# Output projections in seven half-block products: an attention kernel on one TensorE

## The chip, the cores and the metric

The kernel runs on one core of a Trainium2 chip. A core has five engines, each with its own instruction stream: TensorE (PE in the profile) multiplies matrices and writes PSUM, VectorE (DVE) and ScalarE (ACT) work elementwise and may read PSUM, GpSimd (POOL) works elementwise on SBUF, and SyncE (SP) here issues nearly all DMA transfers. The engines wait for one another through semaphores. Each engine runs its own stream strictly in order, so an instruction that waits holds up everything behind it.

The metric is the time of one execution in microseconds on the device. All numbers are f32.

## The reference

One layer: layer norm, cross attention with 8 heads over a context of 3202 rows, a residual, a second layer norm, a small recurrence over time, and a second residual. Cut to what matters here:

```python
x = _layernorm(builder_state, g1, beta1)             # 4096 x 512
base_n = _layernorm(base_state, g1, beta1)           # 3202 x 512
x = residual + _mha(x, base_n, W_qkv, b_qkv, W_o, b_o)   # ends with out @ W_o.T + b_o
xn = _layernorm(x, g2, beta2)
U = (xn @ W_in.T + b_in) @ Bmat
def step(s, u_t):
    s = jax.nn.silu(s @ A.T) + u_t
    return (s, s)
# states over the 4096 rows, then x + states @ Cmat + a row that depends on ctxb
```

The change concerns `out @ W_o.T`: 4096 x 512 by 512 x 512.

## The kernel before

*Stages.* For the first 200 us the kernel normalizes the context and computes keys and values, which go to DRAM. Then comes the attention of 64 units: a unit is 256 queries (a half of a block of 512) by a pair of heads (`hp`, 0 to 3). There are 8 blocks `Q`, and in each but the last the units run pair by pair, both halves of a pair in turn. A unit goes through the context in 13 chunks of 256 keys (`NDC`). At the end, a recurrence over the rows and the last outputs remain.

*One chunk.* `scores` (L1095) is 16 matmul instructions on 64x64 tiles of the array, into one of two PSUM tiles `s`. ACT takes the exponential into a tile `p` of SBUF (`weights`, L1172, `NP` = 15 tiles in a ring). `product` (L1229) multiplies it by the values, 16 instructions, four steps later (`LAG`), and DVE adds `p` into a sum (`add`, L1180). After 13 chunks a unit's output is copied to a tile `o` (L1274), joined (L1278), and scaled by the inverse of the sum (reciprocal L1301, `scale` L1312).

*Projections of the queries.* For the next block these run in `by_sevenths`: the 512x512 product is split into four quarters, and seven products of half size replace eight (Strassen's scheme in Winograd's form). The differences of the weights (`query_weights`) are made once; three to four sums of the other side (`tq`, L1468) are made per block. `seventh` (L364) is one product: 4 matmuls of 128x128 by 128x256, which the profile lists as 8 instructions, because an f32 matmul is two. The seven go in the order `CHAIN` = 1 2 6 5 7 3 4 into two PSUM banks x and y. A bank holds running sums: after some products an engine reads it (`READS`: four by ACT at L1491, three by DVE at L1487) before the next product adds to it.

*Projections of the outputs.* `project` does a half of a block in one piece `outs` (L1561): for each of two tiles of 128 rows, 4 matmuls of 128x128 by 128x512, 16 instructions in all. Then per tile DVE adds the residual (`x1`, L1574), to which POOL has added the bias (`row`, L1555); the second layer norm follows, POOL adds a further row (`mod`, L1578), DVE turns it (`flip`, L441), DMAs move the parts into place (`move`), and PE makes 64 inputs of the recurrence (`inputs`, L1618; `kept`).

*What sets the order.* All work from the attention on is added to a `Plan` as pieces: engine, cost in ns, the pieces it comes after, a due time, and the ring buffers that it takes and gives (`p`, `m` for two PSUM tiles, `x`, `x1`, `o_` and so on). `Plan.order` simulates the engines with these costs and takes, whenever an engine is free, the ready piece that is due first. `SHIFT` moves the due times of a kind of piece by multiples of `STEP` = 2150 ns. For PE, pieces of kind "quarters" (64x64 tiles) and those on the full array are told apart: a change between them costs `ENTER` or `LEAVE`, full-array pieces are kept together (`KEEP`), and a lone one is put off (`ALONE`). The order that comes out is written as the program of each engine; at run time only semaphores decide. The chunks of K and V are loaded by SP 10 and 6 steps ahead.

*The end.* `drain` plans it: the last half's projection (L1881), its rows, a sweep "a" and a sweep "b" of the recurrence over most rows, a recurrence of 20 dependent steps for the last rows (L1966 on ACT, L1969 on DVE), and 16 row tiles that are fetched, added to and stored. Row tiles 0 to `NA` - 1 lie in `alt` tiles, the others in the ring `p`.

Of the kernel before, what the change touches and what calls it, by code (L numbers as in the profile page):

```python
# [20 lines left out]
P = 128  # L21
# [20 lines left out]
NP = 15  # L42
NA = 3
# [28 lines left out]
class Plan:  # L72
# [8 lines left out]
    ENTER, LEAVE = 110, 147  # L81
# [3 lines left out]
    PORT = ("add", "rest", "fold", "gather", "scale", "t", "tq", "tied", "wk", "wv", "wq", "rowv")  # L85

    SHIFT = {
        "row.store": 11.5, "fold": 2, "rows.outs": 0.75, "heads": -12, "sample": -3, "spread": 4.75,
        "query.flip": -11, "states": -5.5, "inverse": 4.75, "extra": 10, "scale": -57.75, "rest": -1,
        "row.mod": -17, "joined0": -14.25, "b": -15, "add.l": -23, "l.stats": -34.75, "last": -4.5,  # L90
        "base": -34.75, "inverse.l": -27, "rows.inputs": 3.5, "maximum": -13.5, "fall": -19, "query.stats": -8,
        "den": 4.5, "row.scaled": 12, "l.h": -7, "row.stats": -9.25,
    }

    def __init__(self, rings, held):
# [19 lines left out]
    def order(self):  # L115
# [26 lines left out]
        while len(out) < len(pieces):  # L142
            for e in self.LATE:
# [24 lines left out]
                free[e] = now + cost  # L168
                if shares(p):
                    port = free[e]  # L170
                heapq.heappush(events, (free[e], 0, p["at"], p))
                heapq.heappush(events, (free[e] + self.LATE[e], 1, p["at"], p))
# [5 lines left out]
            while events and events[0][0] <= now:  # L178
                _, late, _, p = heapq.heappop(events)
                if late:  # L180
                    for g in p["give"]:
                        givers[g] -= 1
# [10 lines left out]
def xattn_ssm_kernel(  # L193
# [886 lines left out]

    def parts_of(t):
# [3 lines left out]
    o_t = {}  # L1085
# [194 lines left out]
    def finish(w, i, d, plan):  # L1280
# [33 lines left out]
        plan.add(("output", i), "ACT", 360, partial(output, w), [("product", i, NDC - 1)], d, ["o_"])  # L1314
# [6 lines left out]
        else:  # L1321
            plan.add(("fold", i), "DVE", 680, partial(fold, w), [("add", i, NDC - 1)], d + 500)
            plan.add(("swap", i), "ACT", 760, partial(swap, w), [("fold", i)], d + 600, ["rd"])
            plan.add(("gather", i), "DVE", 860, partial(gather, w), [("swap", i)], d + 700, [],
                     [("rd", ("swap", i))])
            plan.add(("sums", i), "PE", 300, partial(sums, w), [("gather", i), from_(d + 8 * STEP)], d + 1000,
                     ["m", "m"], acc, "quarters")
            opened = ("den", i, 0)
            for k in range(2):
                plan.add(("den", i, k), "ACT", 450, partial(denominators, k),  # L1330
# [19 lines left out]
    def norm_pieces(plan, ks, gets, d, after, names, gives, wait):  # L1350
# [21 lines left out]
        for t, (k, v) in enumerate(zip(ks, vs)):  # L1372
            plan.add((*k, "stats"), "DVE", 870, partial(stats_, v, gets[t], names[t]),
                     [after[t]] + ([(*ks[0], "stats")] if t else []),
# [1080 lines left out]
```

## Time and profile before

| | |
|---|---|
| Median of 3 runs | 1912.18 us (1912.11 to 1913.63) |
| The profiled execution | 1913.58 us |
| its span, first to last instruction | 1911.7 us |
| granted TensorE clock, mean | 0.998 |
| PE / DVE / ACT / POOL busy | 1895.2 / 1535.3 / 1176.6 / 237.7 us |
| output projections (L1561) on PE | 107.0 us |

A row of the timeline gives start, length, engine, line, operation, the output and input tiles, the shape, and how many instructions were merged (x16); in brackets stands the idle time of the engine just before it and what ended it. A row of a group gives the count, the time that the group kept its engine busy, the mean length of one in ns, and the idle time before them with what ended it. In a window's row stand its length, then per engine the busy time and number of instructions (PE, PEld for weight loads, DVE, ACT, POOL), the granted clock, the share of DMA and GB/s. A row of the waits gives who waited for whom, the total, the number of times and the longest.

### The profile page before, as it was taken

Reading aid. Unit: us, or ns where it says so; the run is one execution under the profiler, and the core shown is the slowest. Engines: PE = TensorE matmul, PEld = TensorE weight load, DVE = VectorE, ACT = ScalarE, POOL = GpSimd, SP = SyncE. Lnnn points to the kernel's source line nnn. Section 1 sums busy time; section 2 is a strip of 40 time slices with the busy share of each in tenths; the row PEclk is TensorE's granted clock in tenths of the full one; section 3 lists DMA queues with packets and bytes.
Section 4 is the critical chain, followed back from the end, with each engine's and each line's share of the span. In section 5 each row is a group of like instructions: output and inputs, shape, how many; then the busy total and the mean of one; then the engine's idle time right before and its main releaser. Section 6 shows DMA issues by size and latency. Waiting matters only on the chain.

```text
span 1911.7 us, 68126 instructions
## 1 busy us (share of the span) xinstructions
PE 1895.2 (99%) x29464; PEld 1352.6 (71%) x29464; DVE 1535.3 (80%) x2084; ACT 1176.6 (62%) x1675; POOL 237.7 (12%) x382
## 2 busy tenths in 40 slices
PE   9999999999999999999999999999999999999997
PEld 5887679766677667766777667766776677766675
DVE  6642699788879889788878887888978887988876
ACT  3242677576666666656757665766756775756653
POOL 6120000001100120011000120012001110011105
PEclk9999999999999999999999999999999999999999
DMA  7554233132422343224413242234322341544577
GB/s 254 156 158 123 63 102 88 45 101 77 110 71 84 92 126 93 81 75 112 110 41 93 81 121 75 82 89 122 101 68 75 96 122 46 160 120 133 175 197 224
DMA packets 260764, 207.50 MB, mean 109 GB/s; under 512 B 94632, under 2 KB 233896, under 8 KB 260460
## 3 DMA queue, kind: packets, MB, share of 16 engines
q1 hardware_dynamic: 256440, 196.48, 36.6%
q10 hardware_dynamic: 4020, 6.62, 1.1%
q8 instruction: 233, 3.82, 0.9%
q14 instruction: 71, 0.58, 0.1%
HBM read 156.32 MB, written 29.88 MB: 97 GB/s over the span
## 4 chain that ended last, share of the span: by engine, by line


## 5 line engine op out<-in xcount | busy, mean ns | idle before, releaser
L1172 ACT ACTIVATE p<-s,shifts 128x1024 f32<-128x1024 f32 (+1 forms) x832 | 892.9, 1082 | 481.1 <-PE s L1095 464.0
L1180 DVE TENSOR_TENSOR acc<-p,acc 128x1024 f32<-128x1024 f32 (+1 forms) x704 | 829.1, 1178 | 119.8 <-ACT p L1172 85.9
L1095 PE MATMUL s<-q,k 64*64 64x256 f32 x12800 | 837.4, 377 | 0.2 <-ACT p L1172 0.2
L1229 PE MATMUL po<-p,v 64*64 64x256 f32 x12800 | 837.4, 377 | 0.0
L1095 PEld LDWEIGHTS s<-q,k 64*64 64x64 f32 x12800 | 499.9, 133 | 199.5 <-ACT p L1172 16.4
L1229 PEld LDWEIGHTS po<-p,v 64*64 64x64 f32 x12800 | 496.4, 133 | 177.1 <-issue 12.9
L1555 POOL TENSOR_TENSOR xr<-xr,rowb 128x512 f32<-128x512 f32 x30 | 41.3, 1390 | 994.3 <-DMA xr<-in_x_dram 467.4
L1301 DVE RECIPROCAL rd<-rd 128x256 f32<-128x256 f32 (+1 forms) x64 | 110.2, 1723 | 23.5 <-ACT rd L1296 23.5
L1561 PE MATMUL pa<-wo,o 128*128 128x512 f32 x240 | 107.0, 599 | 0.0
L1180 DVE TENSOR_TENSOR acc<-p,p 128x1024 f32<-128x1024 f32 x64 | 78.2, 1222 | 10.9 <-ACT p L1172 10.6
L1561 PEld LDWEIGHTS pa<-wo,o 128*128 128x128 f32 x240 | 44.4, 190 | 56.0 <-issue 56.0
L1204 DVE TENSOR_TENSOR acc<-swap,acc 64x256 f32<-64x256 f32 x126 | 56.7, 450 | 8.9 <-ACT swap L1199 7.0
L1166 DVE TENSOR_TENSOR acc<-x,acc 2x256 f32<-2x256 f32 x128 | 55.0, 430 | 2.5
L1199 ACT COPY swap<-acc 64x256 f32<-64x256 f32 x126 | 50.8, 403 | 6.5 <-DVE acc L1187 3.4
L1578 POOL TENSOR_TENSOR xr<-x,modb 128x512 f32<-128x512 f32 x30 | 38.2, 1273 | 116.9 <-DVE x L1574 116.9
L1491 ACT ACTIVATE q<-qx,bias 128x256 f32<-128x256 f32 x42 | 17.6, 471 | 45.8 <-PE qx L364 45.8
L542 DVE TENSOR_TENSOR ks<-pky,ks 128x512 f32<-128x512 f32 x15 | 10.4, 692 | 43.6 <-PE pky L364 28.7
L1362 POOL TENSOR_SCALAR rstd_x<-mv_x 128x1 f32<-128x1 f32 x28 | 6.2, 221 | 313.5 <-DVE mv_x L1359 311.8
L536 ACT ACTIVATE ks<-pkx,bias 128x256 f32<-128x256 f32 x40 | 16.8, 471 | 45.0 <-PE pkx L364 33.6
L1187 DVE TENSOR_TENSOR acc<-acc 128x512 f32<-128x512 f32 x63 | 43.2, 686 | 1.4
L1278 DVE TENSOR_TENSOR o<-po,o 128x256 f32<-128x256 f32 x64 | 27.0, 421 | 12.3 <-ACT o L1274 7.6
L1129 DVE TENSOR_REDUCE m<-sm 128x1 f32<-128x256 f32 x64 | 24.1, 419 | 15.7 <-PE sm L1115 15.2
(283 smaller groups left out, 1588.8 us busy)
## 6 DMA issues: line engine op xcount, KB each, us to landing
k<-kd SPq DMA_DIRECT2D x432, 128.0 KB, 2.4
v<-vd SPq DMA_DIRECT2D x432, 128.0 KB, 2.3
xn<-x SPq DMA_DIRECT2D x448, 32.0 KB, 1.9
xr<-in_x_dram SPq DMA_DIRECT2D x30, 256.0 KB, 3.4
x1d<-xr SPq DMA_DIRECT2D x30, 256.0 KB, 2.5
x<-in_x_dram SPq DMA_DIRECT2D x28, 256.0 KB, 4.0
cx<-in_ctx_dram SPq DMA_DIRECT2D x25, 256.0 KB, 4.3
kd<-ks SPq DMA_DIRECT2D x20, 256.0 KB, 2.3
```

The source lines that it names most:

```text
L1095: nc.tensor.matmul(s[k0 : k0 + HD, a, b, :], kts[(*w["at"][:2], c)][r, b * CK + k0 : b * CK + k0 + HD], q[r], start=True, stop=True, skip_ ...
L1166: nc.vector.tensor_tensor(to[r], t[r], to[r], ALU.add)
L1172: nc.scalar.activation(t[:, :, :nb, :], w["ps"][c][:, :, :nb, :], AF.Exp, bias=w["shift"])
L1180: nc.vector.tensor_tensor(w["acc"][:, :, :nb, :], t[:, :, :nb, :], before[:, :, :nb, :], ALU.add)
L1187: nc.vector.tensor_tensor(acc[:, :, 0, :], acc[:, :, 0, :], acc[:, :, 1, :], ALU.add)
L1199: nc.scalar.copy(w["swap"][r], of[(1 - k) * HD : (2 - k) * HD])
L1204: nc.vector.tensor_tensor(of[r], w["swap"][r], of[r], ALU.add)
L1229: nc.tensor.matmul(w["po"][k][a * HD : (a + 1) * HD, :QU], vts[Q, hp, c][r, b, a * HD : (a + 1) * HD], t[r, a, b, :], start=(c == 0 and b ...
L1301: nc.vector.reciprocal(w["rd"][:, part], (w["pd"] if last else w["rd"])[:, part])
L1555: nc.gpsimd.tensor_tensor(v["x"], v["x"], rowb, ALU.add)
L1561: nc.tensor.matmul(v["pa"], o_t[Q, c, half][:, t * P : (t + 1) * P], wo[:, c, :], start=(c == 0), stop=(c == NC - 1),)
L1578: nc.gpsimd.tensor_tensor(v["x"], v["x1"], modb, ALU.add)
```

## The change

Three things change.

The output projections of blocks 0 to 6 no longer go through `project`, half by half, but through `project_by_sevenths`, once per block of 512 rows, as seven products. The left side (the attention outputs, in quarters: two halves by two pairs of heads) needs four sums on DVE, two of them written over quarters that are not needed any more; the right side (`wo`) needs four differences, made once by POOL (`output_weights`). The seven products go into two PSUM banks, and DVE reads after each of the seven, adding into the residual rows (L1574's four additions per block go). The rows after it (norm, turn, moves, inputs) are in `rows_pieces`, the second half `HALF` = 18 steps behind the first. `project` keeps the first half of the last block; the last half of it is in `drain` as before.

The output tiles lie in pairs of heads, so that two neighbours form a quarter: 6 pairs in place of 12 halves. Five more `alt` tiles hold the differences of `wo`, one half's `x1` and every third `x` tile (the ring `x` grows from 2 to 3), and `p` falls from 15 to 11 tiles.

The planner's costs are set anew (a few in the diff below), `Plan` takes a time `OVER` by which an engine is free before an operation has ended, and `SHIFT` has 65 entries in place of 28. The first half of the next block's query rows is loaded and normalized `EARLY` = 13 steps sooner.

```diff
-NP = 15
-NA = 3
+NP = 11
+NA = 7
+HALF = 18
+EARLY = 13
+OUTS = 0
...
-    ENTER, LEAVE = 110, 147
+    OVER = {"DVE": 80, "ACT": 100}
+    ENTER, LEAVE = 200, 280
...
-        "row.store": 11.5, "fold": 2, "rows.outs": 0.75, "heads": -12, "sample": -3, "spread": 4.75,
...
+        "row.store": 11.5, "fold": 5, "rows.outs": 12.25, "heads": -12, "sample": 1, "spread": -6.25,
...
+        "row.move3": 1, "l.from": -5, "l.copy": -12, "l.states": -8, "l.turn": -4, "row.flip": 4.5,
+        "swap.l": -4, "l.near": 4, "differ": -0.5, "row.load": 12, "add": 16, "rest.l": -8, "den.l": 12,
...
-                free[e] = now + cost
+                free[e] = now + cost - (self.over.get(e, 0) if cost > 200 else 0)
...
+    def x_tile(name):
+
+        x_tiles.append(name)
+        if len(x_tiles) % 3 == 1:
+            return alt_tile(6, name)
+        return xp_.tile([P, 2, H], F32, tag="x", name=name)
...
-        o = o_t[Q, hp, half] = op.tile([P, QU], F32, tag="o", name=f"o_{w['name']}", bufs=12)
+        if hp % 2 == 0:
+            t = op.tile([P, 2, QU], F32, tag="o", name=f"o_{w['name']}", bufs=6)
+            for k in range(2):
+                o_t[Q, hp + k, half] = t[:, k]
+            o_pairs[Q, hp // 2, half] = t
+        o = o_t[Q, hp, half]
...
-            plan.add(("sums", i), "PE", 300, partial(sums, w), [("gather", i), from_(d + 8 * STEP)], d + 1000,
+            plan.add(("sums", i), "PE", 225, partial(sums, w), [("gather", i), from_(d + 8 * STEP)], d + 1000,
...
+        d -= EARLY * STEP
...
+    def output_weights(plan, after, d):
+
+        b11, b21, b12, b22 = quarters(wo)
+        right, tiles = rights, {}
+        right.update(zip("123", (b11, b21, b22)))
+
+        def sum_(k, x, y):
+            if k in "57":
+                tiles[k] = parts_of(alt_tile(3 + "57".index(k), f"to{k}"))
+            right[k] = tiles["57"[k in "74"]][k in "64"]
+            x, y = (right[z] if isinstance(z, str) else z for z in (x, y))
+            nc.gpsimd.tensor_tensor(right[k], x, y, ALU.subtract)
+
+        for i, (k, x, y) in enumerate((("5", b12, b11), ("6", b22, "5"), ("7", b22, b12), ("4", b21, "6"))):
+            plan.add(("to", k), "POOL", 1300, partial(sum_, k, x, y),
+                     [("to", "567"[i - 1])] if i else after, d + i * STEP)
...
+    def project_by_sevenths(plan, Q, d, index):
+
+        index = {(c, half): index[Q, c, half] for c in range(NC) for half in range(2)}
+        v, xs, x1s, left = {}, {}, {}, {}
+        key, k2s = ("outs", Q), [("rows", Q, half) for half in range(2)]
+        kss = [[("row", Q, half * 2 + t) for t in range(2)] for half in range(2)]
+        ats = [[Q * QB + half * QU + t * P for t in range(2)] for half in range(2)]
+
+        def load(half, t):
+            if t == 0:
+                xs[half] = x_tile(f"xr_{ats[half][0]}")
+            at = ats[half][t]
+            nc.sync.dma_start(xs[half][:, t], x[at : at + P, :])
+
+        def row(half, t):
+            nc.gpsimd.tensor_tensor(xs[half][:, t], xs[half][:, t], rowb, ALU.add)
+
+        for half in range(2):
+            for t in range(2):
+                k = kss[half][t]
+                first = (*kss[half][0], "load")
+                plan.add((*k, "load"), "SP", 800, partial(load, half, t),
+                         [first] if t else [from_(d - 6 * STEP)], d - 6 * STEP + 2 * half + t, [] if t else ["x"])
+                plan.add((*k, "row"), "POOL", 1270, partial(row, half, t),
+                         [(*k, "load"), from_(d - 2 * STEP)], d - STEP)
+
+        def parts():
+            return [o_pairs[Q, pair, half] for half in range(2) for pair in range(2)]
+
+        def open_left():
+            a11, a12, a21, a22 = v["a"] = parts()
+            left.update(zip("124", (a11, a12, a22)))
+            left["7"], left["3"] = a21, a12
+
+        def sum_(k):
+            if k == "5":
+                left["5"], left["6"] = parts_of(alt_tile(2, f"so_{Q}"))
+            a11, a12, a21, a22 = v["a"]
+            x, y, op = {
+                "5": (a21, a22, ALU.add), "6": (left["5"], a11, ALU.subtract),
+                "7": (a11, a21, ALU.subtract), "3": (a12, left["6"], ALU.subtract),
+            }[k]
+            nc.vector.tensor_tensor(left[k], x, y, op)
+
+        def product_(k):
+            if k == "1":
+                open_left()
+                v["x"], v["y"] = (
+                    m_tile([P, 512], f"pa{n}_{Q}").rearrange("p (b k) -> p b k", b=2) for n in "xy"
+                )
+            seventh(v["y" if k in "235" else "x"], left[k], rights[k], k in "125")
+
+        def read(k):
+            m, n = (int(z) - 1 for z in READS[k][0])
+            of, cs = v["y" if k in "235" else "x"], slice(n * QU, (n + 1) * QU)
+            if k == "1":
+                x1s[0] = xp_.tile([P, 2, H], F32, tag="x1", name=f"x1_{ats[0][0]}", bufs=1)
+            elif k == "5":
+                x1s[1] = alt_tile(5, f"x1_{ats[1][0]}")
+            t = x1s[m][:, :, cs]
+            nc.vector.tensor_tensor(t, of, xs[m][:, :, cs] if k in "1654" else t, ALU.add)
+
+        def o_of(pair, half):
+            return ("o_", ("output", index[2 * pair, half]))
+
+        def scales(pair, half):
+            return [("scale", index[2 * pair + k, half], 0) for k in range(2)]
+
+        a11, a12, a21, a22 = [(pair, half) for half in range(2) for pair in range(2)]
+        used = {"5": (a21, a22), "6": (a11,), "7": (a11, a21), "3": (a12,)}
+        for k in "5673":
+            after = {"5": scales(*a21) + scales(*a22) + [(*key, "1")], "6": [("so", Q, "5")],
+                     "7": [("so", Q, "5")], "3": [("so", Q, "6"), (*key, "2")]}[k]
+            plan.add(("so", Q, k), "DVE", 690, partial(sum_, k), after, d, ["tq"] if k == "5" else [],
+                     [o_of(*z) for z in used[k]] + ([("tq", ("so", Q, "5"))] if k in "63" else []))
+        before = {"6": "1", "5": "2", "7": "6", "3": "5", "4": "7"}
+        needs = {
+            "1": scales(*a11) + [("to", "4")] + [(*k, "row") for ks in kss for k in ks],
+            "2": scales(*a12) + [(*key, "1")], "4": scales(*a22),
+        }
+        gives = {
+            "1": [o_of(*a11)], "2": [o_of(*a12)], "3": [o_of(*a12)], "4": [o_of(*a22)], "7": [o_of(*a21)],
+            "5": [("tq", ("so", Q, "5"))], "6": [("tq", ("so", Q, "5"))],
+        }
+        last_scale = scales(*a22)
+        for at, k in enumerate(CHAIN):
+            after = needs.get(k, [("so", Q, k)]) + ([("outs.read", Q, before[k])] if k in before else [])
+            plan.add((*key, k), "PE", 1740, partial(product_, k), after + last_scale,
+                     d + STEP * 3 // 4 + at - (plan.ALONE if at > 1 else 0),
+                     ["m", "m"] if k == "1" else [], gives[k])
+            plan.add(("outs.read", Q, k), "DVE", 690, partial(read, k), [(*key, k)], d + at,
+                     {"1": ["x1"], "5": ["x1b"]}.get(k, []), [("m", (*key, "1"))] if k in "34" else [])
+        done = [("outs.read", Q, k) for k in "23"], [("outs.read", Q, k) for k in "74"]
+        for half in range(2):
+            vs = [dict(x=None) for _ in range(2)]
+            free = ("x1b", ("outs.read", Q, "5")) if half else ("x1", ("outs.read", Q, "1"))
+            rows_pieces(plan, Q, half, d + half * HALF * STEP, vs, lambda half=half: (xs[half], x1s[half]), done[half], free, 12)
...
+    def rows_pieces(plan, Q, half, d, vs, tiles, done, free, gate):
...
+        nv = norm_pieces(plan, ks, [lambda t=t: tiles()[1][:, t] for t in range(2)], d + STEP, [done] * 2,
+                         [f"y{r}" for r in at], [], [from_(d + gate * STEP)])
...
+        plan.add((*k2, "inputs"), "PE", 850, inputs, copied + [from_(d + (gate + 12) * STEP)],
+                 d + 16 * STEP, ["m"], [("xn2", xn2)])
...
-            plan.add(("weights", i, c), "ACT", 200 + 861 * part, partial(weights, w, c),
+            plan.add(("weights", i, c), "ACT", 286 + 828 * part, partial(weights, w, c),
...
-                plan.add(("add", i, c), "DVE", 120 + 1120 * part, partial(add, w, c),
+                plan.add(("add", i, c), "DVE", 135 + 1090 * part, partial(add, w, c),
...
-                s=2, m=2, mt=1, o=1, p=NP, acc=3, extra=4, q=3, tq=1, x=2, x1=1, xn2=1, fs=4,
-                xn=1, xh=2, max=2, rd=2, o_=12,
+                s=2, m=2, mt=1, o=1, p=NP, acc=3, extra=4, q=3, tq=1, x=3, x1=1, xn2=1, fs=4,
+                xn=1, xh=2, max=2, rd=2, o_=6, x1b=1,
...
+        output_weights(plan, [from_(24 * STEP)], 24 * STEP)
...
-                project(plan, Q, range(2), d + 4 * STEP, index)
+                project_by_sevenths(plan, Q, d + (4 + OUTS) * STEP, index)
```

More of the change, by code (lines that the diff above doesn't have):

```diff
@@ L1660, in project @@
[L1660 to L1664 removed]
+            plan.add((*k2, "turn"), "PE", 1050, turn, [(*k, "scaled") for k in ks], d + 5 * STEP - now,
+                     ["m", "m", "xn2"], [("xh", (*ks[0], "scaled"))])
@@ L1693, in last_fetch @@
     def last_fetch():
[L1695 removed]
+        t = x_tile("xr_l")
         for g in range(2):
```

161 lines of the change are left out of this document (94 added, 67 removed).

## The prediction

> **What bounds the kernel now.** First the head of the page, then two windows of one block's length, then TensorE's timeline around the operations that the change touches.
>
> ```profile
> span 1911.7 us, 68126 instructions
> PE 1895.2 (99%) x29464; PEld 1352.6 (71%) x29464; DVE 1535.3 (80%) x2084; ACT 1176.6 (62%) x1675; POOL 237.7 (12%) x382
> PE   9999999999999999999999999999999999999997
> PEclk9999999999999999999999999999999999999999
> 547.47:755.94 208.47, 208.47 (x3516) 145.14 (x3512) 176.40 (x226) 137.19 (x189) 21.53 (x32) 1.00 0.33 91
> 755.94:964.42 208.48, 208.48 (x3517) 145.15 (x3513) 177.59 (x230) 137.15 (x189) 20.60 (x32) 1.00 0.33 91
> ```
>
> TensorE (PE) is busy in every slice but the last, at the full granted clock. The two windows run from one block's query projection to the next one's. Both last 208.47 to 208.48 us and PE is busy throughout, while VectorE (DVE) is busy 176 to 178 of them, ScalarE (ACT) 137 and GpSimd (POOL) 21. Busy alone would not prove a bound, since overlapping matmuls always look busy. The starts in the timeline do. Here is one output projection of 256 rows (L1561) among the attention chunks:
>
> ```profile
> 687.48 1.04 PE L1095 MATMUL s<-q,k 64*64 64x256 f32 x16
> 688.45 7.13 PE L1561 MATMUL pa<-wo,o 128*128 128x512 f32 x16
> 695.52 1.09 PE L1229 MATMUL po<-p,v 64*64 64x256 f32 x16
> 696.43 1.04 PE L1095 MATMUL s<-q,k 64*64 64x256 f32 x16
> 697.30 1.04 PE L1229 MATMUL po<-p,v 64*64 64x256 f32 x16
> ```
>
> An attention chunk of 16 instructions takes its turn every 0.87 us (696.43 to 697.30), although each is listed with 1.04: the last 0.17 is the drain, which the next chunk covers. So PE hands over without a pause, and a block costs what its PE work costs. Saved PE work is saved time there, one for one, as long as nobody else makes PE wait.
>
> The Trainium skill ("Trainium Kernel Development and Optimization", Performance Expectations) says that matmul busy time is a bad measure of the distance to the roofline and that LDWEIGHTS busy is a good one. By it PEld's 71% would leave 29% of slack, another engine would set the pace, and the sum below would be about nothing (the fourth rival). The even starts speak against that here.
>
> **The change part by part.** *Output projections.* Per block two pieces of 16 instructions go. From 687.48 to 697.30 are 9.82 us, which hold three chunks and the piece: 9.82 - 3 x 0.87 = 7.21 us for a half, with the cost of going from 64x64 tiles to the full array and back. A block pays 2 x 7.21 = 14.42.
>
> What comes is the same helper (`seventh`, L364) that projects the queries in seven products. Its rows in one block:
>
> ```profile
> 1589.30 1.91 PE L1095 MATMUL s<-q,k 64*64 64x256 f32 x32
> 1591.13 1.99 PE L364 MATMUL qx<-xn,wq 128*128 128x256 f32 x8
> 1592.96 1.89 PE L364 MATMUL qy<-xn,wq 128*128 128x256 f32 x8
> 1594.69 1.89 PE L364 MATMUL qx<-tq,sq 128*128 128x256 f32 x8
> 1596.51 1.09 PE L1229 MATMUL po<-p,v 64*64 64x256 f32 x16
> 1597.54 1.99 PE L364 MATMUL qy<-tq,sq 128*128 128x256 f32 x8
> 1599.37 1.89 PE L364 MATMUL qx<-xn,sq 128*128 128x256 f32 x8
> 1601.09 1.89 PE L364 MATMUL qy<-xn,sq 128*128 128x256 f32 x8
> 1602.82 1.89 PE L364 MATMUL qx<-xn,wq 128*128 128x256 f32 x8
> 1604.64 1.09 PE L1229 MATMUL po<-p,v 64*64 64x256 f32 x16
> 1605.55 1.04 PE L1095 MATMUL s<-q,k 64*64 64x256 f32 x16
> 1606.42 1.04 PE L1229 MATMUL po<-p,v 64*64 64x256 f32 x16
> ```
>
> 1589.30 to 1606.42 is 17.12 us, with five chunks in it (the x32 counts twice): 17.12 - 5 x 0.87 = 12.77 for seven products in two stints of full-array work (three, a chunk, four). Inside a stint a product follows after 1.73 (1592.96 to 1594.69). Seven of them are 12.11, so the two stints cost 0.66 to enter and leave, 0.33 each. With k stints a block pays 12.11 + 0.33k: 12.44 for one, 12.77 for two, 13.10 for three, and 14.42 for seven, where the gain is exactly gone.
>
> Which k? Products 6, 5, 7, 3 and 4 each wait until VectorE has read an earlier product from the same bank, and 6 also for two new sums that start only after product 1. After product 1 VectorE owes three operations of 0.69 (sum 5, sum 6, read 1), 2.07 us, while PE has only product 2, 1.73 us. So a gap after {1, 2} is certain, to be filled by one or two chunks that are needed anyway. After it each product has only one read of 0.69 to wait for under a product of 1.73. The query chain, the nearest row, breaks once. I take k = 2: 14.42 - 12.77 = 1.65 us per block, 7 x 1.65 = **11.55 us**. Ends: 13.9 (k = 1), 9.2 (k = 3), 0 (k = 7).
>
> *VectorE.* The prices, and what VectorE does during the chain above:
>
> ```profile
> L1574 DVE TENSOR_TENSOR x<-pa,xr 128x512 f32<-128x512 f32 x30 | 20.7, 689 | 19.5 <-PE pa L1561 12.9 <-POOL rstd_y L1363 4.2 <-POOL nm_y L1364 1.8
> L1468 DVE TENSOR_TENSOR tq<-xn,tq 128x512 f32<-128x512 f32 x7 | 4.8, 691 | 0.2
> L1180 DVE TENSOR_TENSOR acc<-p,acc 128x1024 f32<-128x1024 f32 x640 | 784.9, 1226 | 113.7 <-ACT p L1172 83.9
> L1301 DVE RECIPROCAL rd<-rd 128x256 f32<-128x256 f32 x62 | 108.4, 1749 | 23.5 <-ACT rd L1296 23.5
> 1596.99 2.48 DVE L1180 TENSOR_TENSOR acc<-p,acc 128x1024 f32<-128x1024 f32 x2
> 1601.36 0.69 DVE L1487 SCALAR_TENSOR_TENSOR q<-qx,q 128x512 f32<-128x512 f32 x1 [1.88 <-PE qx L364]
> 1603.02 0.69 DVE L1487 SCALAR_TENSOR_TENSOR q<-qy,q 128x512 f32<-128x512 f32 x1 [0.97 <-PE qy L364]
> 1607.81 1.23 DVE L1180 TENSOR_TENSOR acc<-p,acc 128x1024 f32<-128x1024 f32 x1 [4.10 <-ACT p L1172]
> ```
>
> Four left sums and seven reads come, four additions (L1574) go: 7 more operations of 0.69, 4.8 us a block, 176.4 + 4.8 = 181 of 207 us. VectorE stays under PE. The new work also falls where VectorE runs dry: while PE does projections no scores arrive, ACT makes no weights and the adds stop, with idle times of 1.88, 0.97 and 4.10 us here. Costed at nothing; were that cover gone, 4.8 us a block would lie ahead of the adds, and the 4 weight tiles that a product lags behind would hold about 8 us of it (4 chunk pairs at 208.47 / 104 = 2.0 us).
>
> *GpSimd and the queues.*
>
> ```profile
> L1578 POOL TENSOR_TENSOR xr<-x,modb 128x512 f32<-128x512 f32 x30 | 38.2, 1273 | 116.9 <-DVE x L1574 116.9
> ```
>
> The four weight differences run once, 4 x 1.27 us, the price of an addition of the same shape, on an engine 12% busy, and the first use is a block away: nothing. If they held up VectorE for their whole length it would be 5 us of VectorE, once. The row loads, bias additions, stores and the 32 moves of a block stay the same in number on POOL and SP; the second half's loads move ahead and all four bias additions now come before product 1. SP also carries the K and V loads, so a store or move that waits holds those back. V tiles are asked for six chunks ahead, 12 us of cover; without it PE waits by what a move is late. I take nothing, with at worst a few tenths of a us per block.
>
> *Buffers.* p falls from 15 to 11. A product lags four steps, so four or five tiles wait for products and a few for adds: nothing. The pairs of o (12 halves as before) are all held until the chain; four pairs are full then and the next block opens its third new pair only at its fifth unit, some 100 us on: nothing.
>
> *Dates.* They change the order, not the work. In the steady part there is no idle PE time to win. At the end there is a chain: the last projection, then a recurrence of 20 dependent steps (L1969).
>
> ```profile
> 1856.57 3.70 PE L1881 MATMUL yb<-wo,o 128*128 128x512 f32 x8
> 1876.40 0.21 DVE L1969 SCALAR_TENSOR_TENSOR scan<-scan,zl 128x32 f32<-128x32 f32 x1 [0.55 <-ACT scan L1966]
> 1895.17 0.22 DVE L1969 SCALAR_TENSOR_TENSOR scan<-scan,zl 128x32 f32<-128x32 f32 x1 [0.30 <-ACT scan L1966]
> 1896.37 0.21 DVE L1969 SCALAR_TENSOR_TENSOR scan<-scan,zl 128x32 f32<-128x32 f32 x1
> 1902.64 0.20 DVE L1969 SCALAR_TENSOR_TENSOR scan<-scan,py_o 128x32 f32<-128x32 f32 x1
> 1904.36 0.20 DVE L1969 SCALAR_TENSOR_TENSOR scan<-scan,py_o 128x32 f32<-128x32 f32 x1
> ```
>
> From the last projection's start (1856.57) to the end of the span are 55.1 us. First to last step of the recurrence is 27.96 us, 19 distances of 1.47. At the short distance of 1.20 (1895.17 to 1896.37) it would be 22.8, a gain of 5.2; at the long one of 1.72 (the last two rows) 32.7, a loss of 4.7. The row lies in the middle, so I take 0 and keep both ends.
>
> *Sum.* 11.55 us off. The profiled execution took 1913.58 us (span 1911.7), 1.4 above the median of 1912.18; the sum is the same for both, so from the median 1912.18 - 11.55 = **1900.6 us**.
>
> **The rivals.**
>
> 1. *PE waits in the chain (the other side).* Place: the products after {1, 2}, if the order leaves no chunk where a read is late.
>
> ```profile
> PE qy L364 <- DVE q L1487: 1.2, 1, 1.2
> ```
>
> In the chain of waits PE stood before a query product for a VectorE read once in seven blocks, 1.2 us: it can happen, and it speaks against often. In the query chain ACT does four of the seven reads; here VectorE does all, behind adds of 1.23 and reciprocals of 1.75. Price: 2.07 - 1.73 + 1.75 = 2.1 before product 6, and 0.69 + 1.23 - 1.73 = 0.2 before each of four later ones: 2.9 us a block, 7 x (2.9 - 1.65) = 8.8 on top, 1921. It decides from 1.65 us of waiting per block. The Trainium skill ("TensorEngine Tiling (Array Packing)", PSUM Bottleneck) advises using both ScalarE and VectorE to empty PSUM; the change puts all seven reads on one, and no run so far shows what that costs.
>
> 2. *The chain falls into single products.* k = 6 to 7 gives 14.09 to 14.42 per block, 1909.9 to 1912.2. For it: five waits on a loaded engine. Against it: the query chain's four products in a row.
>
> 3. *More is won.* One stint, or a full-array piece such as the small input projection sharing a stint, and a shorter end: 13.9 plus up to 4, 1894.
>
> 4. *PE is not the bound*, and the saving does not arrive: 1912.2. Against it, the even starts.
>
> **How the numbers follow.** A difference of 0.2% (3.8 us) is about what a measurement of this kernel can tell from none: under 1908.4 is faster, over 1916 slower. Forecast (two or three stints, end within its bounds, 1895 to 1907): 0.58. Third rival: 0.13. Together faster, 0.71. Second rival 0.09 and fourth 0.03 are no change. First rival 0.17, of which 0.04 pays back only the gain and 0.13 is slower. So same is 0.16, slower 0.13. The range goes from the third rival's 1894 to just past no gain at all, 1913; that leaves out the slower 0.13 and some 0.04 below.
>
> **What would show it.** Right: groups of 8 instructions at L364 with `wo` sums 1.73 apart, in two stints per block with chunks after the second product; a block (from one query chain to the next) of 206.8 us; no new idle PE row against the read's line; VectorE about 181 us per block; the same 55 us from the last projection to the end. Wrong: idle PE before the sixth or fifth product, a block near or over 208.5, `p` or K/V loads appearing among PE's releasers, or a longer recurrence at the end.

## The result, and the profile after

The changed kernel takes 1977.63 us (1971.79 to 1978.87) where the kernel before took 1912.14 in the same set: 1.0335 times as long, 95% interval 1.0314 to 1.0357. It is 65 us slower, where 11.6 us less was forecast. The profiled execution took 1977.17 us. First the head of its page, then a window from the start of one block's output chain to the start of the next (span, then busy time and instructions of TensorE, its weight loads, VectorE, ScalarE and GpSimd, then clock, DMA share and GB/s).

```profile
span 1975.4 us, 68723 instructions
PE 1911.6 (97%) x29632; PEld 1384.7 (70%) x29632; DVE 1558.8 (79%) x2133; ACT 1171.0 (59%) x1675; POOL 270.7 (14%) x386
PE   9999999999999999999999989999999999999997
427.31:646.30 218.99, 210.79 (x3541) 150.44 (x3537) 180.17 (x235) 136.57 (x189) 25.20 (x32) 0.98 0.31 86
```

A block lasts 218.99 us in place of 208.47. TensorE's digits look the same but for one 8, and VectorE is as busy as forecast (180 us, 181 forecast). Only the window's row tells: PE is busy for 210.79 of 218.99 us, so it is idle for 8.2 us of this block, and the clock is 0.98.

Did the saving arrive? TensorE's timeline of one output chain and one query chain:

```profile
646.30 1.99 PE L378 MATMUL pax<-wo,o 128*128 128x256 f32 x8
648.13 1.89 PE L378 MATMUL pay<-wo,o 128*128 128x256 f32 x8
649.95 1.09 PE L1252 MATMUL po<-p,v 64*64 64x256 f32 x16
650.97 1.99 PE L378 MATMUL pax<-to,so 128*128 128x256 f32 x8
...
654.62 1.09 PE L1252 MATMUL po<-p,v 64*64 64x256 f32 x16
655.65 1.99 PE L378 MATMUL pax<-to,o 128*128 128x256 f32 x8
...
661.02 1.09 PE L1118 MATMUL s<-q,k 64*64 64x256 f32 x16
661.94 1.04 PE L1252 MATMUL po<-p,v 64*64 64x256 f32 x16
...
778.52 1.99 PE L378 MATMUL qx<-xn,wq 128*128 128x256 f32 x8
...
790.81 1.09 PE L1252 MATMUL po<-p,v 64*64 64x256 f32 x16
791.72 1.04 PE L1118 MATMUL s<-q,k 64*64 64x256 f32 x16
```

It did, though not in the stints that were forecast (a stint is a stretch of full-array work without a chunk in it). The outputs run as {1, 2}, a chunk, {6, 5}, a chunk, {7, 3, 4}: 646.30 to 661.94 is 15.64 us with three chunks in it, 15.64 - 3 x 0.87 = 13.03. The queries now run in one stint: 778.52 to 791.72 less one chunk is 12.33. The prediction's counts began a chunk earlier, and so had 0.10 in them for the step from chunk to full array (687.48 to 688.45 is 0.97, not 0.87); with it these are 13.13 and 12.43, together 25.56 us, where before two halves and a query chain of two stints took 14.42 + 12.77 = 27.19. That is 1.63 us a block; 1.65 were forecast, with two stints for the outputs and two for the queries. The outputs alone saved 1.29; the other 0.34 comes from the queries' one stint, which the prediction did not count on. And nothing waits inside the chain.

Counting every instruction at the pitch it has when nothing waits (1.73 / 8 us in the full array, 0.87 / 16 in 64x64 tiles), from 201 us to the last projection, gives the whole balance (us):

| | before | after | difference |
|---|---|---|---|
| full-array instructions | 201.6 | 190.1 | -11.5 |
| going in and out of them, waits in them | 8.1 | 7.9 | -0.2 |
| 64x64 instructions | 1427.4 | 1427.4 | 0 |
| time lost in the 64x64 stretches | 17.8 | 90.4 | +72.6 |
| from the last projection to the end | 55.2 | 57.9 | +2.8 |

The differences add up to the 63.7 us between the spans (1911.7 and 1975.4). So 72.6 us were lost in attention, whose work the change leaves as it was. Who ends the waits there, from the list of waits of the changed kernel (waiting engine and tile, line, what ended the wait; us in all, times, longest):

```profile
ACT swap L1222 <- DVE acc L1210: 78.0, 33, 5.3
PE po L1252 <- DVE o L1306: 38.4, 13, 5.3
DVE st_x L1387 <- DMA x<-in_x_dram: 26.2, 11, 5.0
```

The list of the kernel before has no wait of TensorE for `o`. For `swap` it has:

```profile
ACT swap L1199 <- DVE acc L1187: 3.4, 11, 1.3
```

ScalarE's waits need not cost anything: 53.0 us of them for `swap` remain in the run below that has neither large hole. TensorE's waits do. L1306 is the join: VectorE's addition that empties the one PSUM bank of `po` at the end of a unit. Three holes, stretches in which TensorE stands, come in each of the steady blocks, and two of them are large. The first, in the timelines of TensorE, VectorE and GpSimd:

```profile
624.00 1.74 PE L1252 MATMUL po<-p,v 64*64 64x256 f32 x27 [2.92 <-DVE o L1306]
...
615.68 1.94 DVE L1203 TENSOR_TENSOR acc<-p,p 128x1024 f32<-128x1024 f32 x1 [0.28 <-ACT p L1195]
617.54 2.91 DVE L1227 TENSOR_TENSOR acc<-swap,acc 64x256 f32<-64x256 f32 x2
620.46 1.82 DVE L1189 TENSOR_TENSOR acc<-x,acc 2x256 f32<-2x256 f32 x2
622.39 1.23 DVE L1203 TENSOR_TENSOR acc<-p,acc 128x1024 f32<-128x1024 f32 x1
623.53 0.42 DVE L1306 TENSOR_TENSOR o<-po,o 128x256 f32<-128x256 f32 x1
...
615.00 6.58 POOL L1604 TENSOR_TENSOR xr<-xr,rowb 128x512 f32<-128x512 f32 x4 [101.17 <-DMA xr<-in_x_dram]
```

GpSimd adds the bias to all four row tiles back to back from 615.00 to 621.58. In that time VectorE's operations on two SBUF tensors take longer: an addition 1.94 us and, at 622.39 when GpSimd is done, 1.23; two gathers 2.91. The join comes 3 us late, and PE stands. The planner had set the four additions 2.4 us apart, after the join; but GpSimd waits for nothing except the loads, which landed sooner than planned. The second hole, in the timelines of TensorE, VectorE and of SyncE's DMA issues (the duration of a row is the time from first to last issue):

```profile
514.63 1.98 PE L1252 MATMUL po<-p,v 64*64 64x256 f32 x16 [4.56 <-DVE o L1306]
...
506.19 0.70 DVE L1387 BATCH_NORM_STATS2 st_x<-x 128x6 f32<-128x512 f32 x1 [3.53 <-DMA x<-in_x_dram]
...
509.61 0.69 DVE L1387 BATCH_NORM_STATS2 st_x<-x 128x6 f32<-128x512 f32 x1 [1.87 <-DMA x<-in_x_dram]
...
485.98 3.42 SPq L467 DMA_DIRECT2D xn<-x  x4
...
498.46 3.71 SPq L467 DMA_DIRECT2D xn<-x  x4
...
503.34 0.42 SPq L1425 DMA_DIRECT2D x<-in_x_dram  x1
```

VectorE waits 3.53 + 1.87 us for the next query rows and the join stands behind it in its queue. The load was issued at 503.34, after sixteen moves (four rows of four, from 485.98) and the K and V loads between them: 17.4 us, for which the planner reckons 10.4 and no K and V loads. The third hole is 0.7 us: TensorE waits for ScalarE's exponential, which stands behind `swap`, and `swap` waits for VectorE's fold. (The expectations call it 1.1 us; they count from the start of the last instruction before a hole, 0.38 us more than the idle time in the brackets.)

```profile
561.17 1.09 PE L1118 MATMUL s<-q,k 64*64 64x256 f32 x16 [0.72 <-ACT p L1195]
```

The holes also cost clock. Windows of the changed kernel, in order: behind the 4.56 us hole, after that, behind the 2.92 us hole above, and behind another one of 2.92 us (400.41 to 403.33):

```profile
514.63:521.00 6.37, 6.37 (x68) 3.82 (x72) 6.11 (x7) 1.67 (x3) 0.00 (x0) 0.56 0.10 29
521.00:528.00 7.00, 7.00 (x138) 4.60 (x133) 3.99 (x5) 5.71 (x7) 0.00 (x0) 1.00 0.08 14
624.00:630.00 6.00, 6.00 (x112) 4.30 (x116) 5.65 (x8) 2.23 (x2) 0.00 (x0) 1.00 0.01 3
403.33:407.00 3.67, 3.67 (x44) 2.39 (x48) 3.53 (x6) 0.00 (x0) 0.00 (x0) 0.61 0.00 0
```

Over 6.37 us at 0.56 PE starts 68 matmuls, in the next 7.00 us 138. The Trainium skill ("TensorE: Matmul & The Clock Gate", HAM oscillation) says that an idle gap of more than some 3.4 us brings the clock down to half. The trace agrees only in part: of the eleven large holes, the five from 3.17 us up each came with 3.4 or 6.8 us at half clock, but so did two shorter ones (2.92 us at 400.41 and 2.54 at 837.49), while four of 2.42 to 2.92 us did not. In all 45.5 us of the span ran at half clock, before 6.8.

### The profile page after: what moved, and what is told of

It is laid out like the page before. It is cut to its first block, busy times and chain, and to the rows that moved or that the text cites. A ratio compares the mean times of both kernels' runs of the same rounds, so it can differ in the third digit from the quotient of the medians.

```text
span 1975.4 us, 68723 instructions
## 1 busy us (share of the span) xinstructions
PE 1911.6 (97%) x29632; PEld 1384.7 (70%) x29632; DVE 1558.8 (79%) x2133; ACT 1171.0 (59%) x1675; POOL 270.7 (14%) x386
## 4 chain that ended last, share of the span: by engine, by line
## 5 line engine op out<-in xcount | busy, mean ns | idle before, releaser
L1252 PE MATMUL po<-p,v 64*64 64x256 f32 x12800 | 929.9, 381 | 38.6 <-DVE o L1306 38.4
L1118 PE MATMUL s<-q,k 64*64 64x256 f32 x12800 | 921.1, 379 | 4.9 <-ACT p L1195 4.8
L1252 PEld LDWEIGHTS po<-p,v 64*64 64x64 f32 x12800 | 546.7, 134 | 231.5 <-DVE o L1306 46.2
L1118 PEld LDWEIGHTS s<-q,k 64*64 64x64 f32 x12800 | 541.6, 134 | 207.1 <-ACT p L1195 23.4
L1391 POOL TENSOR_SCALAR rstd_x<-mv_x 128x1 f32<-128x1 f32 x28 | 17.3, 618 | 474.5 <-DVE mv_x L1388 377.2
L1227 DVE TENSOR_TENSOR acc<-swap,acc 64x256 f32<-64x256 f32 x126 | 63.8, 506 | 3.0 <-ACT swap L1222 1.2
L1189 DVE TENSOR_TENSOR acc<-x,acc 2x256 f32<-2x256 f32 x128 | 62.7, 490 | 1.4
L556 DVE TENSOR_TENSOR ks<-pky,ks 128x512 f32<-128x512 f32 x15 | 10.4, 692 | 43.4 <-PE pky L378 28.6
L1387 DVE BATCH_NORM_STATS2 st_x<-x 128x6 f32<-128x512 f32 x28 | 19.3, 689 | 26.3 <-DMA x<-in_x_dram 26.2
L1306 DVE TENSOR_TENSOR o<-po,o 128x256 f32<-128x256 f32 x64 | 26.8, 419 | 14.2 <-ACT o L1302 14.0
L1180 ACT ACTIVATE x<-sm,shifts 128x256 f32<-128x256 f32 x64 | 26.8, 471 | 12.4 <-DVE shifts L1174 12.3
L1324 ACT ACTIVATE rd<-pd 128x128 f32<-128x128 f32 x126 | 33.5, 274 | 0.3 <-PE pd L1280 0.3
```

What stands on the lines that cost most here:

```text
L1118: nc.tensor.matmul(s[k0 : k0 + HD, a, b, :], kts[(*w["at"][:2], c)][r, b * CK + k0 : b * CK + k0 + HD], q[r], start=True, stop=True, skip_ ...
L1189: nc.vector.tensor_tensor(to[r], t[r], to[r], ALU.add)
L1227: nc.vector.tensor_tensor(of[r], w["swap"][r], of[r], ALU.add)
L1252: nc.tensor.matmul(w["po"][k][a * HD : (a + 1) * HD, :QU], vts[Q, hp, c][r, b, a * HD : (a + 1) * HD], t[r, a, b, :], start=(c == 0 and b ...
L1324: nc.scalar.activation(to, of, AF.Copy, accum_out=rises[:, 3 * i + k : 3 * i + k + 1])
```

## The experiments

The theory after the result: the work is no more than forecast, but the two halves' loads, additions and moves, which used to come apart, now come together, and GpSimd and SyncE run them at another time than the planner thinks. The rivals: the renewed dates alone do it, or VectorE simply has no time left for the new work.

**One cause at a time.** The row bias left out, the loads of query rows two and three put ahead of the moves, and both.

```diff
         def row(half, t):
-            nc.gpsimd.tensor_tensor(xs[half][:, t], xs[half][:, t], rowb, ALU.add)
+            return
```

```diff
+            for Q in range(2, NQB):
+                for t in (2, 3):
+                    p = pieces["query", Q, t, "load"]
+                    out.pop(next(i for i, o in enumerate(out) if o is p))
+                    out.insert(next(i for i, o in enumerate(out) if o["name"] == ("row", Q - 2, 2, "move0")), p)
```

> Leaves out: POOL's addition of the output bias to the residual rows of blocks 0 to 6 (row does nothing); the order of all other instructions is the same. Port theory (four POOL additions in a row slow VectorE's two-input operations beside them, so the join that frees PE's bank comes late): the six PE holes of 2.8 to 3.3 us near 400, 621, 837, 1058, 1277 and 1495 us go, 18 us and some 3 us of lowered clock, 1956 us; the six holes of 1.2 to 5.7 us near 510 to 1602 stay. Load theory: 1977, all holes stay. Rival, that VectorE is behind because of the products' added work: within 3 us of 1977.

> Moves the load of the second half of the next query rows, in blocks 2 to 7, ahead of the 16 moves that it stands behind on SP; nothing else. Load theory (VectorE's statistics wait for that load, and the join behind them comes late): the holes near 510, 729, 946, 1165, 1385 and 1602 us go, 24 us and some 12 us of lowered clock, 1942 us; the holes near 400 to 1495 stay. Port theory: 1977. Rival (VectorE too loaded): over 1970, since the statistics would then be late anyway.

> Leaves out POOL's addition of the output bias in blocks 0 to 6 and moves the query loads ahead of the moves. Load and port theory together: 57 us off, 1920 us, with the holes of 1.1 us before the query chain left. Rival (VectorE too loaded by the added sums and reads): over 1960.

Measured (in brackets the ratio to the kernel before in the same set, and its 95% interval): 1947.76 (1.0187, 1.0164 to 1.0209), 1942.88 (1.0158, 1.0136 to 1.0181) and 1912.80 us (1.0004, 0.9994 to 1.0013). Of the two large holes the first run has the second only, the second run the first only, the third neither. From 1977.63 the two take 29.9 and 34.7 us, together 64.6; both at once take 64.8. They add up, so they are two causes, and with both gone the kernel is where it was before. The forecasts of 1956 and 1920 were some 8 us too high.

**Dates or products?** The seven products with the planner's numbers of before, and the kernel before with the changed kernel's numbers.

```diff
-EARLY = 13
+EARLY = 0
...
-    OVER = {"DVE": 80, "ACT": 100}
-    ENTER, LEAVE = 200, 280
+    OVER = {}
+    ENTER, LEAVE = 110, 147
...
```

with `SHIFT` and the durations likewise; for the other run the same lines the other way round, with the lines of `Plan` that use `OVER`.

> The seven products, pairs and rings of the change with the dates and costs that the planner had before (SHIFT, costs, ENTER and LEAVE, no OVER, EARLY 0). If the dates are the cause and the products are sound: 1900 to 1912 us. If the products' work on VectorE is the cause: over 1940 us, with joins late in every block.

> The kernel before, with the seven products left out and the changed kernel's dates, durations and costs of a switch in its planner (each half of the rows still loads, adds its bias and is multiplied by itself). Theory (the products bring the four row loads, four bias additions and sixteen query moves of a block together, and that makes the holes): the time stays near the kernel before, 1908 to 1920 us, with no hole over 2 us at the join in the steady blocks. Rival (the renewed dates alone crowd the queues): 1930 to 1960 us, with join holes of 3 us or more in every block.

Measured: 1952.84 (1.0214, 1.0197 to 1.0231) and 1944.64 us (1.017, 1.0154 to 1.0185). With the old dates the place of the holes is another one, from its list of waits:

```profile
PE pu L1705 <- DMA xn<-x: 20.4, 6, 4.4
PE po L1246 <- DVE o L1300: 4.2, 5, 0.9
```

The input projection now waits for the moves, 2.6 to 4.4 us in each of six blocks: SyncE is late again, for another customer. The time lies in the range of the rival that blames the products' work on VectorE (over 1940), but that rival's sign, a late join in every block, is missing: the join waited five times, 0.9 us at most. The dates alone make no join hole over 1.24 us, as the theory said, but the time is 25 us above its forecast and in the rival's range. From the start of the last query chain (1591.13 before, 1603.32 here) and of the last projection (1856.57, 1885.65) one reads +12 us over the blocks and +17 in what follows, with single waits such as

```profile
PE pu L1631 <- DMA xn<-x: 5.3, 2, 3.1
PE qy L376 <- DVE q L1500: 6.3, 5, 1.5
```

So both parts cost when alone, and the rival about the dates is right in that. The products are even slower with the new dates (1977.63) than with the old ones. What each date costs in the end part was not taken apart.

**Nothing left out, other places.** If the holes come from where the additions fall, moving them must do as much as leaving them out. The early query loads stay; the four row loads and additions go directly ahead of the next query load:

```diff
+            for Q in range(NQB - 1):
+                for p in [pieces["row", Q, t, n] for n in ("load", "row") for t in range(4)]:
+                    out.pop(next(i for i, o in enumerate(out) if o is p))
+                    at = ("query", Q + 2, 0, "load") if Q < NQB - 2 else ("add", 8 * Q + 8, 4)
+                    out.insert(next(i for i, o in enumerate(out) if o["name"] == at), p)
```

> Nothing left out. Only places in the planner's list move: the loads of query rows two and three of a block go ahead of the sixteen moves, as in the run with the early query load, and the four row loads and their four bias additions go directly ahead of the next query load, some 4 to 8 us later, so that GpSimd adds after the join. Theory (the holes are made by where these land, not by the amount of work): 1913 us (1910 to 1920), both kinds of hole gone, about as with the additions left out (1912.8). Rival (the four additions cost VectorE their time wherever they stand, since it has none to spare): 1925 to 1945, with join holes of 2 us or more at other places.

Measured: 1914.48 us (1.0012, 1.0003 to 1.0021). A window of one block, and the timelines of VectorE and GpSimd:

```profile
549.08:756.58 207.50, 206.78 (x3540) 149.37 (x3536) 179.56 (x235) 136.29 (x189) 27.87 (x32) 1.00 0.33 91
```

```profile
603.70 0.85 DVE L1238 TENSOR_TENSOR acc<-swap,acc 64x256 f32<-64x256 f32 x2
...
606.65 0.42 DVE L1317 TENSOR_TENSOR o<-po,o 128x256 f32<-128x256 f32 x1
...
608.98 7.87 DVE L1214 TENSOR_TENSOR acc<-p,acc 128x1024 f32<-128x1024 f32 x4
...
609.26 8.72 POOL L1615 TENSOR_TENSOR xr<-xr,rowb 128x512 f32<-128x512 f32 x4 [106.27 <-DMA xr<-in_x_dram]
```

The gathers take 0.85 for two again (2.91 above) and the join is in time. The price has not gone: GpSimd's additions now stretch four of VectorE's to 7.87 us (4 x 1.22 alone), but there VectorE has time to spare. The block is 207.50 us, 0.97 less than before. It is placement, not the amount of work: a lack of time on VectorE is refuted as the cause of the 65 us.

**What is left.** Three more orders go for the remaining waits. First the fold of every unit in blocks 1 to 6 directly behind its last addition; then that for six units only, GpSimd's weight differences moved to 410 us and the last store sooner; then the differences moved to 197 us and six reciprocals behind the fold. The lines of the third, in which `move` takes a piece of the list behind (1) or ahead of (0) another:

```diff
+            for Q in range(1, NQB - 1):
+                move(("fold", 8 * Q + 5), ("add", 8 * Q + 5, NDC - 1), 1)
+                move(("inverse", 8 * Q + 4, 0), ("fold", 8 * Q + 5), 1)
+            for k in "5674":
+                move(("to", k), ("query", 1, 0, "factors"), 0)
+            move(("stored1", L - 1), ("l.out", 0), 0)
```

> The kernel of the run before in this set, and on VectorE the fold of a unit goes directly behind its last addition, ahead of the scale and the fall of the unit before. Theory (ScalarE's swap waits for the fold and holds the weights of the next scores behind it, 1.1 us once in a block): the 1.1 us holes shrink to about 0.4 us, six blocks by 0.7 us give 4 us less than that run, about 1909 us. Rival (the swap's wait only passes to the scale, which then releases the output's tile late): no difference within 2 us, or up to 5 us more.

> Nothing left out; the kernel with the query loads early and the rows after the next query load (1914.5 us), with three more places moved: GpSimd's four differences of output weights from 221 us to behind the first block's row additions (410 us); the fold directly behind its unit's last addition in the six units alone that showed the 1.1 us wait; and the last row's store ahead of the last half's on SyncE. Theory (each is a wait of TensorE or of the end with nothing late behind it): 1.3 us at the join at 227.6 us, six folds by 0.6 us and 1.2 us at the end give some 6 us, 1908 to 1910 us, below the kernel before (1912.2). Rival (what is moved is made up by a wait next to it, as with all folds moved, which took the 1.1 us holes away and was 4 us slower): 1913 to 1919.

> Nothing left out; the run before with two places changed: GpSimd's four output weight differences go ahead of the first query factors (about 197 us, before the steady units need VectorE) in place of 410 us, where together with the four row additions they kept VectorE's additions at 2.08 us for seven in a row and opened a hole of 2.42 us at 415 us; and in six units the reciprocal of the unit before goes behind the fold. Theory (holes are placement alone): the 2.4 us hole goes and the six 0.5 us waits go, 1908.5 us (1907 to 1911). Rival (the differences take VectorE's time at 197 us too, or the reciprocal's delay releases a tile late): 1913 us or more.

Measured: 1918.68 (1.0036, 1.0024 to 1.0048), 1913.13 (1.0005, 0.9996 to 1.0014) and 1911.15 us (1.0001, 0.9992 to 1.001). The first took the 0.7 us holes away and was 4 us slower than the run before it, as the rival said: its steady block takes 208.2 us, 0.7 more, with no single new hole over 0.5 us. The second missed the range of its theory (1908 to 1910) and the third just missed it (1907 to 1911). The second shows the largest stretching of all, VectorE and GpSimd at 400 us:

```profile
399.87 14.57 DVE L1224 TENSOR_TENSOR acc<-p,acc 128x1024 f32<-128x1024 f32 x7
...
399.99 8.88 POOL L1625 TENSOR_TENSOR xr<-xr,rowb 128x512 f32<-128x512 f32 x4 [109.15 <-DMA xr<-in_x_dram]
```

Seven additions in a row take 2.08 us each on the mean, and GpSimd's own 2.2 in place of 1.27. Single operations out of these rows show how:

```profile
402.19 2.25 POOL L1625 TENSOR_TENSOR xr<-xr,rowb 128x512 f32<-128x512 f32 x1
403.41 2.12 DVE L1224 TENSOR_TENSOR acc<-p,acc 128x1024 f32<-128x1024 f32 x1
404.40 2.25 POOL L1625 TENSOR_TENSOR xr<-xr,rowb 128x512 f32<-128x512 f32 x1
405.63 2.11 DVE L1224 TENSOR_TENSOR acc<-p,acc 128x1024 f32<-128x1024 f32 x1
```

They end at 404.44, 405.53, 406.65 and 407.74, in turn, 1.1 us apart: about half of each row's length passes before the other engine's operation has ended. The Trainium skill ("SBUF — State Buffer", SBUF: two separate sides) says that the two engines share one pair of ports, which an operation with two SBUF inputs holds for its whole length. The ends in turn agree. A turn is a little shorter than an operation alone (1.1 against 1.22 and 1.27 us), and why is not shown.

**The rival of the prediction, made on purpose.** Would PE wait inside the chain if it were not broken up? One chunk moved out of it, then both, with left sums 5 and 6 sooner.

```diff
+            for Q in range(NQB - 2):
+                i = 8 * Q + 8
+                move(("so", Q, "6"), ("outs", Q, "1"), 1)
+                move(("so", Q, "5"), ("outs", Q, "1"), 1)
+                move(("add", i + 1, 2), ("outs.read", Q, "2"), 1)
+                move(("product", i + 1, 0), ("outs", Q, "4" if True else "5"), 1)
+                if True:
+                    move(("product", i + 1, 1), ("product", i + 1, 0), 1)
```

These are the lines of the run with one stint; the run with two has `False` in both places.

> Nothing left out. The run before with the reciprocal at its old place, and in six blocks products 1, 2, 6 and 5 in one stint: the chunk of the next unit between them goes behind product 5, the left sums 5 and 6 go ahead of the additions on VectorE, and one addition of the next unit goes behind the reading of product 2. Theory (holes are placement alone and a stint costs 0.33 us to enter and leave): six times 0.3 us at the queries and six times 0.33 us for the stint less, 1907 to 1909 us. Rival (VectorE's readings then come too late inside the chain, the place at which the prediction feared them): a wait of 0.5 to 1 us before product 6 or 5 in each block, 1911 to 1917 us.

> Nothing left out. As the run with two stints, and the second chunk also goes behind product 4, so that the seven products of six blocks stand in one stint of 12.3 us, as the query projections' do. Theory: another six times 0.33 us, 1905 to 1907 us. Rival (VectorE must read seven results, make four left sums and has the additions of two units behind them in 12.3 us): it comes late at the next join or fold, 1911 to 1920 us.

Measured: 1911.0 (1.0, 0.9991 to 1.0009) and 1920.2 us (1.0052, 1.0038 to 1.0066). Both missed the ranges of their theories (1907 to 1909, 1905 to 1907). TensorE's timeline and list of waits of the one with a single stint:

```profile
634.71 1.89 PE L407 MATMUL pay<-to,so 128*128 128x256 f32 x8
638.00 1.99 PE L407 MATMUL pax<-to,o 128*128 128x256 f32 x8 [1.40 <-DVE x L1678]
639.83 1.89 PE L407 MATMUL pay<-wo,o 128*128 128x256 f32 x8
642.49 1.99 PE L407 MATMUL pax<-to,o 128*128 128x256 f32 x8 [0.77 <-DVE x L1678]
```

```profile
PE pax L407 <- DVE x L1678: 13.2, 12, 1.5
```

Products 7 and 4 wait for VectorE's readings, which stand behind additions. From 634.71 to 638.00 are 3.29 us and from 639.83 to 642.49 2.66, against 1.73 without a wait: 2.5 us a block. In two stints (1, 2, 6, 5, then 7, 3, 4) nothing waits before products 6 and 5, and the one wait left, before product 4 (`PE pax` for `DVE x`, 2.2 us in six blocks), takes what the six stints saved (6 x 0.33 us). So the changed kernel's two chunks between the products are well placed.

No version is faster than the kernel before. The nearest is the one with two stints: the medians of 11 and 15 runs are 1911.0 and 1910.9, and its profiled execution has a span of 1907.3, where the shortest of the kernel before in that set is 1908.0.

## Why the prediction was wrong

- *TensorE's saving*: the size was right, 11.5 us less full-array work, and 0.33 us a stint held. The choice of two stints for the outputs was not: there were three, for which the prediction's own sum is 9.2. That 11.5 came out is luck, because the new dates joined the queries' two stints into one. That "a gap after {1, 2} is certain" was wrong too: with the left sums 5 and 6 ahead of the additions on VectorE, products 1, 2, 6 and 5 ran without a wait.
- *VectorE costed at nothing*: right for the product chain as it was built, and 180 us a block as forecast. A wait for its readings, the first rival's, showed only where the chunks were taken out: 2.5 us a block, 2.9 forecast. But it stood before products 7 and 4, and the forecast had most of it before product 6, so the near agreement is luck.
- *GpSimd and the queues*: this step failed. "I take nothing, with at worst a few tenths of a us per block" counted the operations ("the same in number"), not when they run. The prediction even noted that "all four bias additions now come before product 1", and gave that no price. They cost 64.8 us, some 11 us a block over six blocks: the additions at the join 29.9, the loads behind the moves 34.7. The weight differences, also costed at nothing, showed as 0.9 us at one join (227.96 us), gone when they ran at 197 us.
- *The rows that spoke against it* were in the trace of before, in the timelines of GpSimd and VectorE:

```profile
602.31 2.34 POOL L1555 TENSOR_TENSOR xr<-xr,rowb 128x512 f32<-128x512 f32 x1 [2.66 <-DMA xr<-in_x_dram]
...
603.56 1.81 DVE L1166 TENSOR_TENSOR acc<-x,acc 2x256 f32<-2x256 f32 x2
...
624.59 0.84 DVE L1166 TENSOR_TENSOR acc<-x,acc 2x256 f32<-2x256 f32 x2
```

One bias addition at the end of a unit had doubled both engines' times; four together at that place could have been priced from these rows.

- *Dates costed at nothing*: wrong as a principle. "They change the order, not the work" holds, but the order is what cost: alone the dates are 32 us slower. The end chain grew by 2.8 us, within its bounds.
- *The rivals*: the first has the right pair of engines (PE waits for VectorE) and the wrong place and price, 1921. The loss came through GpSimd and SyncE, which stood in no rival, so no range from these cases could hold 1977.63. The others did not occur.
- *Where the saving went*: with the two large holes gone and nothing left out, the steady block is 0.97 us shorter where 1.65 were forecast. The third hole is nearly all of the difference: in the run that moved six folds, the blocks without it take 206.97 us, 1.50 less than before. Over the whole of the run with other places (1914.48 us), counted at the pitch as in the table, full-array work takes some 11.8 us less, and some 12 us more are lost elsewhere: 3.3 before the first query chain, 3.2 in the six blocks from there, 1.4 from the last of these chains to the last projection and 4.2 from there to the end. What makes the waits at the beginning and at the end was not settled.

## What to carry to other kernels

Before an engine or a queue is costed at nothing, look up where its operations fall, and not only how many there are: an engine that is 12% busy can stop the critical one if its work lands in the few microseconds in which the critical one waits for a third. A planner's list fixes only the order on each queue; an operation that waits for a load alone runs when the load lands, and all that stands behind a late load in its queue is late too. Compare operations of one line inside and outside another engine's work: their durations show a shared resource that no busy share shows.

## What was not expected of the hardware

GpSimd's and VectorE's additions on two SBUF tensors stretch each other: VectorE's from 1.22 to 2.12 us (the last six of seven in a row) and its small gathers from 0.43 to 1.45, GpSimd's from 1.27 to 2.25. They end in turn, so that a small operation is held up by the large one beside it. Behind a hole of 4.56 us TensorE ran at 0.56 of its clock for 6.37 us, which costs 2.8 us more (6.37 x 0.44). Of two holes of 2.92 us in the same execution one was followed by half clock and the other was not: a late join can cost more than its wait, and its length alone does not tell.
